# A transformer block on one core: the first stage put in program order on three engines, and a cleared scratch tile between scatters

## The chip, the cores and the metric

The kernel runs on one core of a Trainium2 chip. A core has five engines that work beside each other: TensorE (PE in the profile, with its weight load as PEld), VectorE (DVE), ScalarE (ACT), GpSimd (POOL) and SyncE (SP). Each takes its own instructions strictly in the order in which the build laid them out, and waits at an instruction until what it needs has been signalled. SyncE here only issues DMAs; GpSimd also issues the DMAs that scatter rows to computed addresses. PSUM is the memory that TensorE writes to, SBUF the one that all engines work in.

The metric is the device time of one execution in microseconds, and lower is better. Seven runs of the kernel before have a median of 507.76 us (505.48 to 509.74).

## What is computed

One block over 2048 tokens of width 256: an attention over a sliding window of 64, then a mixture of 16 experts with 4 chosen per token, each behind a layer norm that is shifted and scaled by a small product (`c` with `w_mod`).

```python
mod = (silu(c) @ wmod).reshape(1, 6, 1, -1)        # sa, ca, ga, sb, cb, gb
h = layernorm(x) * (1 + ca) + sa
q, k, v = split(h @ w_qkv.T)                       # 16 heads of 16
s = q k^T / 4 over chunks of 64 queries, 128 keys  # this chunk and the one before, masked
x = x + ga * (softmax(s) @ v) @ w_out.T
h = layernorm(x) * (1 + cb) + sb
probs = softmax(abs((h @ ru.T) * silu(h @ rg.T)))  # 16 experts
idx = top 4 of probs + extra_bias;  w = 1 + probs[idx] * extra_scale[idx]
y = sum over the 4 experts: w * ((silu(h @ Wg.T) * (h @ Wu.T)) @ Wd.T)
z = (silu(h @ Sg.T) * (h @ Su.T)) @ Sd.T           # the shared expert
x = x + gb * (y + z)
```

## The kernel before

**Tiles.** The tokens are cut into four blocks of 512 (NB = 4, TB = 512), each of four tiles of 128 (NT). The width of 256 is two halves of 128 (KC = 2).

**First stage.** All loads are issued on SyncE at L263 to L287, in the order of the lines: `c`, block 0 of x, the first third of w_mod, the weights of queries, keys and values, the rest. A one-time fill of constants (masks, identity, counters) runs on VectorE and GpSimd at L114 to L187. `shift_scale` (L299) makes shift and scale of a norm by eight small matmuls (two passes each) into `ps_mod` and two VectorE copies into `mod`.

**front(b)** (L352) prepares a block: `norm_t` (L227) takes four bn_stats and bn_aggr on VectorE (L233, L234), a square root on ScalarE (L236), four normalisations `xn` (L241), eight transposes on TensorE (L249) and two ScalarE passes into `hT` (L250); then come queries (L363, split into even and odd heads by VectorE at L368 and ScalarE at L369), keys (L374, copied by ScalarE at L378) and values (L393, copied at L397 to L399). It is a generator: each `yield` is a point at which the loop that drives it turns to something else.

**Attention** runs over 64 units (16 for a block, UNITS), driven by the loop at L692. A unit is one of four head pairs of a half block. `scores(u)` (L443) fills PSUM for two units, mask first (L450), then eight products (L456). `softmax(u)` takes the row maximum on VectorE (`top`, L472). Even units subtract it there (L482) and take one Exp on ScalarE (L485); odd ones take four Exps with a bias and a running sum (L477). `total` sums the even ones (L490), `turn_p` transposes (L497, copied by L499), and once in four units `spread`, `turn_s`, `values` and `heads_out` make the weighted values (L507, L519, L533, L546). While a block's units run, the loop advances by one step per unit `front` of the next block and `back` of the one before; `gates` takes the place of `back` in the first block.

**back(b)** (L556) applies the output weights (`ps_a`), adds to x (L569), does the second norm into a tile `row` (two buffers), routes (L581 to L658) and appends 16 entries to `sends`: four choices times four tiles.

**send** (L664) takes one entry: a GpSimd copy into the last column of the row's tile, from an operand that VectorE has written (`tops` of the unit two ahead in the loop; in the tail of the stage a result of the shared expert), and then a scatter of 128 rows to `slots` in HBM (L673). The copy is there only to hold the scatter back: the column is spare. A copy into a row waits until the scatter that last read that tile has landed.

**After the last unit** the expert weights `wgu` (5632 KB) are loaded over the attention's buffers (L724). The shared expert of blocks 0 to 2 (`shared`, L403, driven by `beside`) covers the rest of routing. Then the fill counts are known (`ps_n`, L747), SyncE writes 16 blank tiles behind the filled slots (L805) and loads the rows of each expert tile (`xr`, L820); the first of these loads waits for every scatter and every blank. The shared expert of block 3 runs meanwhile. 79 expert tiles follow, each with transposes, two products and an accumulating scatter (L831 to L878), and at the end the sums are loaded, added to x and stored.

**Order.** A scheduler in the build, which weighs readiness and program order by its own estimates, decides the order on each engine. Nothing in the kernel before overrides it.

Of the kernel before, what the change touches and what calls it, by code (L numbers as in the profile page):

```python
# [8 lines left out]
F32 = mybir.dt.float32  # L9
BF16 = mybir.dt.bfloat16  # L10
# [7 lines left out]
P = 128  # L18
E = 256
KC = E // P  # L20
HD = 16
W = 64
TB = 512
NT = TB // P
# [6 lines left out]
def adaln_block_kernel(  # L31
# [17 lines left out]
    nc = tc.nc  # L49
    S = x.shape[0]  # L50
    NB = S // TB
# [11 lines left out]
    RW = E + NE + 4  # L63
# [9 lines left out]
    xs = []  # L73
# [37 lines left out]
        return w.rearrange("(k p) n -> p k n", p=P)  # L111


    ident = const.tile([P, P], F32, name="ident")  # L114
    make_identity(nc, ident)
    eps_b = const.tile([P, 1], F32, name="eps_b")
# [110 lines left out]
    def norm_t(pool, psum, xb, half, dst, xn=None):  # L227

        mv = pool.tile([P, NT, 2], F32, tag="mv", name="mv")
        rstd = pool.tile([P, NT], F32, tag="rstd", name="rstd")  # L230
        for t in range(NT):
            st = pool.tile([P, 6], F32, tag="st", name="st")
            nc.vector.bn_stats(st, xb[:, t, :])  # L233
            nc.vector.bn_aggr(mv[:, t, :], st)  # L234
        yield
        nc.scalar.activation(rstd, mv[:, :, 1], AF.Sqrt, bias=eps_b[:, 0:1])  # L236
        nc.vector.reciprocal(rstd, rstd)
        if xn is None:
            xn = pool.tile([P, NT, E], F32, tag="xn", name="xn", bufs=1)
        for t in range(NT):  # L240
            nc.vector.tensor_scalar(  # L241
                xn[:, t, :], xb[:, t, :], mv[:, t, 0:1], rstd[:, t : t + 1],
                ALU.subtract, ALU.mult,
            )
        for k in range(KC):
            yield
            ps = psum.tile([P, NT, P], F32, tag="mm", name="ps_xt")
            for t in range(NT):
                nc.tensor.transpose(ps[:, t, :], xn[:, t, k * P : (k + 1) * P], ident)  # L249
            nc.scalar.activation(  # L250
                dst[:, k, :], ps[:, :, :].rearrange("p t q -> p (t q)"), AF.Identity,
                bias=mod[:, 3 * half, k : k + 1], scale=mod[:, 3 * half + 1, k : k + 1],
            )
# [87 lines left out]
    with ExitStack() as actx:  # L341
# [6 lines left out]
        k_before = None  # L348
# [3 lines left out]
        def front(b):  # L352
            nonlocal k_before, ve_next
            yield from norm_t(wa, ps_mm, xs[b], 0, hT[b])


            qz = next(q_ring).rearrange("p (k n h q) -> p k n h q", k=KC, h=2, q=W)
            kT = next(k_ring).rearrange("p (k n) -> p k n", k=KC)
            for m in range(KC):
                yield  # L360
                ps = ps_mm.tile([P, TB], F32, tag="mm", name="ps_q")
                for k in range(KC):
                    nc.tensor.matmul(  # L363
                        ps, lhsT=wqkv[:, k, m * P : (m + 1) * P], rhs=hT[b][:, k, :],
                        start=(k == 0), stop=(k == KC - 1),
                    )
                by_chunk = ps[:, :].rearrange("p (n q) -> p n q", q=W)
                nc.vector.tensor_scalar(qz[:, m, :, 0, :], by_chunk, parity[:, 0:1], None, ALU.mult)  # L368
                nc.scalar.mul(qz[:, m, :, 1, :], by_chunk, parity[:, 1:2])  # L369
            for m in range(KC):  # L370
                yield
                ps = ps_mm.tile([P, TB], F32, tag="mm", name="ps_k")
                for k in range(KC):
                    nc.tensor.matmul(  # L374
                        ps, lhsT=wqkv[:, k, E + m * P : E + (m + 1) * P], rhs=hT[b][:, k, :],
                        start=(k == 0), stop=(k == KC - 1),
                    )
                nc.scalar.copy(kT[:, m, W:], ps)  # L378
            if k_before is None:
                nc.vector.memset(kT[:, :, 0:W], 0.0)  # L380
            else:
                nc.vector.tensor_copy(kT[:, :, 0:W], k_before[:, :, TB:])
            k_before = kT


            window = []
            for t in range(NT):
                yield
                vo = next(v_ring["vo"])
                ve, ve_next = ve_next, next(v_ring["ve"])  # L390
                ps = ps_mm.tile([P, E], F32, tag="mm", name="ps_v")
                for k in range(KC):
                    nc.tensor.matmul(  # L393
                        ps, lhsT=hT[b][:, k, t * P : (t + 1) * P], rhs=wqkv[:, k, 2 * E :],
                        start=(k == 0), stop=(k == KC - 1),
                    )
                nc.scalar.copy(vo, ps)  # L397
                nc.vector.tensor_copy(ve[W:P], ps[0:W])
                nc.vector.tensor_copy(ve_next[0:W], ps[W:P])  # L399
                window += [ve, vo]  # L400
            heads[b] = qz, kT, window

        def shared(b, hidden, psum):  # L403

            hs = []
            for j in range(SJ):
                n = min(P, SH - j * P)
                h = hidden()
                hs.append(h)
                pg, pu = psum(), psum()  # L410
                for ps, w in ((pg, sg), (pu, su)):
                    for k in range(KC):
                        nc.tensor.matmul(  # L413
                            ps[0:n], lhsT=w[:, k, j * P : j * P + n], rhs=hT[b][:, k, :],
                            start=(k == 0), stop=(k == KC - 1),
                        )
                    yield hs[-2][:, 0:1] if j else None
                nc.scalar.activation(h[0:n], pg[0:n], AF.Silu)
                nc.vector.tensor_tensor(h[0:n], h[0:n], pu[0:n], ALU.mult)
            for t in range(NT):  # L420
                ps = psum()[:, 0:E]
                for j in range(SJ):
                    n = min(P, SH - j * P)
                    nc.tensor.matmul(  # L424
                        ps, lhsT=hs[j][0:n, t * P : (t + 1) * P], rhs=sd[0:n, j, :],
                        start=(j == 0), stop=(j == SJ - 1),
                    )
                nc.vector.tensor_tensor(xs[b][:, t, :], ps, xs[b][:, t, :], ALU.add)
                yield xs[b][:, t, 0:1]

        UNITS = 4 * 2 * KC
        probs, tops, sums, turned, scale, av, outs = {}, {}, {}, {}, {}, {}, {}

        def where(u):

# [24 lines left out]
        def softmax(u):  # L464

            g, r = divmod(u, 4)
            s = probs[u]
            if r == 0:
                sums[g] = wa.tile([P, 4, 4], F32, tag="sum", name="sum")
            alone = r % 2 == 1  # L470
            top = tops[u] = wa.tile([P, 4], F32, tag="top", name="top", bufs=6)
            nc.vector.tensor_reduce(top, s, AX.X, ALU.max, negate=alone)  # L472
            sm = wa.tile([P, 4, 2 * W], F32, tag="sm", name="sm", bufs=4)
            probs[u] = sm
            if alone:
                for n in range(4):
                    nc.scalar.activation(  # L477
                        sm[:, n, :], s[:, n, :], AF.Exp, bias=top[:, n : n + 1],
                        accum_out=sums[g][:, n, r : r + 1],
                    )  # L480
                return
            nc.vector.tensor_tensor(  # L482
                sm, s, top[:, :].unsqueeze(2).to_broadcast([P, 4, 2 * W]), ALU.subtract
            )
            nc.scalar.activation(sm, sm, AF.Exp)  # L485
# [175 lines left out]

        sends = []

        def send(after=None):  # L664

            at, row, t, i = sends.pop(0)  # L670
            if after is not None:
                nc.gpsimd.tensor_copy(row[0 : after.shape[0], t, RW - 1 : RW], after)  # L672
            ins = nc.gpsimd.indirect_dma_start(  # L673
                out=slots[:, :],
                out_offset=bass.IndirectOffsetOnAxis(ap=at[:, t, i : i + 1], axis=0),
# [5 lines left out]


        heads = {}
        shift_scale(ps_mm, 0)
        for _ in front(0):
            pass
        last = NB * UNITS
        scores(0)
        softmax(0)
        softmax(1)  # L690
        nexts, ends = iter(()), gates(wa, ps_mm)
        for u in range(last + 3):  # L692
            if u % UNITS == 0 and u // UNITS + 1 < NB:
# [24 lines left out]
            next(nexts, None)  # L718
            for _ in range(2 if r == 3 else 1):
                next(ends, None)  # L720

            for _ in range(min(len(sends), 2 if r == 3 else 1)):
                send(tops[min(u + 2, last - 1)][:, 0:1])
        nc.sync.dma_start(out=wgu, in_=w_gu_t.rearrange("(k p) e n -> p k e n", p=P))  # L724


# [8 lines left out]
        side = beside()  # L735
        for _ in ends:
            next(side, None)
            done = next(side, None)
            for _ in range(min(len(sends), 2)):
                send(done)  # L740
        while sends:
            done = next(side, None)
            send(done)


        ps = ps_mm.tile([P, NE], F32, tag="mm", name="ps_n")
# [224 lines left out]
```

## Time and profile before

The profiled execution took 507.14 us, of which 505.4 us are the span from its first to its last instruction.

| what | value |
|---|---|
| median of 7 runs | 507.76 us |
| profiled execution, its span | 507.14 us, 505.4 us |
| TensorE busy | 459.5 us (91%) |
| VectorE busy | 337.9 us (67%) |
| ScalarE busy | 226.3 us (45%) |
| GpSimd busy | 203.0 us (40%) |
| first row maximum (`top`) starts | 29.12 us |
| `wgu` load issued | 213.97 us |
| first expert product (`pgu`) | 284.02 us |
| granted TensorE clock, mean | 0.972 |

A timeline row reads: start in us, busy us, engine, line and operation, what is written from what, shapes, count; in brackets the idle time of the engine just before the row and what ended it. A row of the windows reads: the stretch and its length, then busy us of PE, PEld, DVE, ACT and POOL with the number of instructions in brackets, the granted TensorE clock, the busy share of the DMA engines and GB/s. Times of an engine in a row overlap at their edges, so that rows back to back start closer together than they last.

### The profile page before, as it was taken

The numbers are of one execution on the slowest core, as the hardware profiler recorded it, in microseconds if no ns is written. First come the engines' busy times: TensorE is split into PE (matmuls) and PEld (weight loads), VectorE is DVE, ScalarE is ACT, GpSimd is POOL, SyncE is SP. The second block draws the span as 40 slices with busy tenths as digits, with TensorE's granted clock in tenths as the row PEclk, the third lists the DMA queues.
The fourth block names the chain that finished last, engine by engine and source line by source line (L and its number), as shares of the span: only waits on it lengthen the run. The fifth ranks groups of instructions, "written<-read, shape, count | busy, mean of one in ns | idle before, by whom it ended". The sixth has DMA issues, their size and how long they took to land.

```text
span 505.4 us, 9573 instructions
## 1 busy us (share of the span) xinstructions
PE 459.5 (91%) x2921; PEld 324.1 (64%) x2921; DVE 337.9 (67%) x913; ACT 226.3 (45%) x623; POOL 203.0 (40%) x224
## 2 busy tenths in 40 slices
PE   3999979998998899899999999999999999999900
PEld 3575757666766677556553777777777777777700
DVE  5599789789969898755324466666666666666625
ACT  2377687958866868733001233333333333333200
POOL 2002000007701750246363066566666556666630
PEclk9999999999999899899999999999999999999965
DMA  8978000002200220095126487777777657665478
GB/s 281 320 153 285 21 1 3 0 1 82 92 10 12 91 80 2 23 408 195 46 90 224 102 150 131 114 112 117 104 116 108 105 104 111 118 100 58 57 217 314
DMA packets 52565, 58.88 MB, mean 117 GB/s; under 512 B 16363, under 2 KB 48331, under 8 KB 52171
## 3 DMA queue, kind: packets, MB, share of 16 engines
q1 hardware_dynamic: 36435, 35.72, 24.8%
q0 software_dynamic: 14448, 19.41, 22.3%
q10 hardware_dynamic: 1632, 3.15, 1.6%
q8 instruction: 24, 0.39, 0.3%
q14 instruction: 26, 0.21, 0.2%
HBM read 29.90 MB, written 28.35 MB: 115 GB/s over the span
## 4 chain that ended last, share of the span: by engine, by line
PE 42%; DMA 37%; DVE 12%; ACT 4%; issue 3%; DVEq 0%; SPq 0%; POOLq 0%; ACTq 0%
DMA sum<-y,xr 34%; PE pz L413 8%; PE pz L424 4%; PE pt L497 4%; PE s L456 3%; DVE top L472 3%; PE ps_q L363 3%; PE av L533 3%; PE pgu L849 2%; PE ps_a L564 2%; PE ps_k L374 2%; DMA got<-sum 2%; ACT sm L477 2%; PE s L450 2%; PE ps_xt L249 1%
## 5 line engine op out<-in xcount | busy, mean ns | idle before, releaser
L878 POOL DMA_INDIRECT sum<-y,xr x79 | 122.2, 1547 | 92.1 <-DVE y L877 34.4
L849 PE MATMUL pgu<-wgu,xT 128*128 x316 | 106.5, 460 | 0.4 <-DVE xT L837 0.4
L871 PE MATMUL py<-wd,hT 88*128 x316 | 81.4, 379 | 0.1
L673 POOL DMA_INDIRECT slots<-row,at x64 | 63.4, 991 | 32.5 <-POOL row L672 13.6
L833 ACT ACTIVATE xT<-px,mod 128x128 f32<-128x128 f32 x79 | 36.1, 457 | 81.1 <-PE px L831 80.9
L849 PEld LDWEIGHTS pgu<-wgu,xT 128*128 128x128 f32 x316 | 53.8, 190 | 17.4 <-ACT xT L833 0.6
L865 DVE COPY hT<-ph 88x256 f32<-88x256 f32 x79 | 33.2, 421 | 39.8 <-PE ph L863 39.8
L871 PEld LDWEIGHTS py<-wd,hT 88*128 88x128 f32 x316 | 53.6, 190 | 4.8 <-DVE hT L865 0.5
L672 POOL COPY row<-top 128x1 f32<-128x1 f32 x44 | 8.3, 200 | 110.0 <-DVE sr L606 62.2
L855 ACT ACTIVATE h<-pgu 128x176 f32<-128x176 f32 x79 | 25.1, 318 | 59.3 <-PE pgu L849 59.3
L477 ACT ACTIVATE sm<-s,top 128x128 f32<-128x128 f32 x128 | 45.8, 371 | 11.1 <-DVE top L472 11.0
L497 PE MATMUL pt<-ident,sm 128*128 128x128 f32 x256 | 41.3, 284 | 7.3 <-ACT sm L485 6.0
L837 DVE TENSOR_SCALAR xT<-px,mod 128x128 f32<-128x128 f32 x79 | 32.4, 410 | 22.0 <-ACT xT L833 21.9
L499 ACT COPY pT<-pt 128x512 f32<-128x512 f32 x64 | 37.5, 593 | 19.8 <-PE pt L497 19.4
L472 DVE TENSOR_REDUCE top<-s 128x4 f32<-128x512 f32 x64 | 42.2, 683 | 3.2 <-PE s L456 2.8
L456 PEld LDWEIGHTS s<-wgu 32*128 32x128 f32 x512 | 31.7, 186 | 15.9 <-issue 15.5
L877 DVE TENSOR_TENSOR y<-py,gate 128x256 f32<-128x256 f32 x79 | 33.6, 425 | 11.7 <-PE py L871 1.0
L497 PEld LDWEIGHTS pt<-ident,sm 128*128 128x128 f32 x256 | 29.3, 143 | 15.6 <-ACT sm L485 6.9
L456 PE MATMUL s<-wgu 32*128 32x128 f32 x512 | 38.9, 285 | 0.0
L863 PEld LDWEIGHTS ph<-ident,h 128*88 128x88 f32 x158 | 19.4, 123 | 21.9 <-issue 13.5
L856 DVE SCALAR_TENSOR_TENSOR h<-h,by,pgu 128x176 f32<-128x176 f32 x79 | 30.3, 384 | 1.3 <-ACT h L855 1.3
L831 PE MATMUL px<-ident,xr 128*128 128x128 f32 x158 | 30.4, 273 | 0.1
(169 smaller groups left out, 710.0 us busy)
## 6 DMA issues: line engine op xcount, KB each, us to landing
xr<-slots SPq DMA_DIRECT2D x79, 138.0 KB, 2.6
wgu<-in_w_gu_t SPq DMA_DIRECT2D x1, 5632.0 KB
sum<-blank SPq DMA_DIRECT2D x2, 2176.0 KB
wd<-in_w_down_t SPq DMA_DIRECT2D x1, 2816.0 KB
slots<-blank SPq DMA_DIRECT2D x17, 138.0 KB, 2.4
x<-in_x SPq DMA_DIRECT2D x4, 512.0 KB
got<-sum SPq DMA_DIRECT2D x4, 512.0 KB, 6.9
got<-sum ACTq DMA_DIRECT2D x4, 512.0 KB
```

The lines of the kernel that those rows point to most:

```text
L413: nc.tensor.matmul(ps[0:n], lhsT=w[:, k, j * P : j * P + n], rhs=hT[b][:, k, :], start=(k == 0), stop=(k == KC - 1),)
L456: nc.tensor.matmul(probs[u + i][:, n, :], lhsT=qz[at, m, ch].rearrange("p h q -> p (h q)"), rhs=kT[at, m, ch * W : (ch + 2) * W], start=False,
L472: nc.vector.tensor_reduce(top, s, AX.X, ALU.max, negate=alone)
L477: nc.scalar.activation(sm[:, n, :], s[:, n, :], AF.Exp, bias=top[:, n : n + 1], accum_out=sums[g][:, n, r : r + 1],)
L497: nc.tensor.transpose(pt[:, n, :], p[:, n, :], ident)
L499: nc.scalar.copy(turned[u], pt)
L673: ins = nc.gpsimd.indirect_dma_start(out=slots[:, :], out_offset=bass.IndirectOffsetOnAxis(ap=at[:, t, i : i + 1], axis=0), in_=row[:, t, ...
L833: nc.scalar.activation(xT[b][:, 0, :], ps[:, 0, :], AF.Identity, bias=mod[:, 3, 0:1], scale=mod[:, 4, 0:1],)
L849: nc.tensor.matmul(ps, lhsT=xT[b][:, k, :], rhs=wgu[:, k, bass.ds(e, 1), :].rearrange("p e n -> p (e n)"), start=(k == 0), stop=(k == KC - 1),
L871: nc.tensor.matmul(ps, lhsT=hT2[b][:, c2, :], rhs=wd[:, c2, bass.ds(e, 1), :].rearrange("p e n -> p (e n)"), start=(c2 == 0), stop=(c2 == 1),)
L877: nc.vector.tensor_tensor(y, ps, gate[:, 1, :], ALU.mult)
L878: nc.gpsimd.indirect_dma_start(out=sums_of[b % NA][:, :], out_offset=bass.IndirectOffsetOnAxis(ap=xr[b][:, E + NE : E + NE + 1].bitcast(I3 ...
```

## The change

There are two parts.

The first stage, from the identity to the values of block 0, is built under a manual schedule for TensorE, VectorE and ScalarE, which keeps its instructions in program order on these three engines. The program's order is changed with it: two steps of `front(0)` (the norm) come before `shift_scale`; then the transposes, queries of half 0 and keys of half 0; then `scores(0)`, `softmax(0)` and `softmax(1)`; then queries and keys of half 1 and all values. In `front` the loops over queries and keys become one loop over halves, for every block. The bn_stats of the first norm of blocks 1 to 3 are kept in program order as well.

In `send` the copied operand is replaced: with `paced` set, GpSimd clears a scratch tile of 128 x 1024 bf16 (one buffer) and copies two of its columns into the spare column of two of the row's four tiles, t and the one two away from it. The last loop sends without pacing. `tops` is no longer kept, and its tile has four buffers in place of six.

```diff
+    first_order = ctx.enter_context(ExitStack())
+    first_order.enter_context(tc.manual_schedule(
+        engines={mybir.EngineType.PE, mybir.EngineType.DVE, mybir.EngineType.Activation}
+    ))
     ident = const.tile([P, P], F32, name="ident")
...
-            nc.vector.bn_stats(st, xb[:, t, :])
+            ins = nc.vector.bn_stats(st, xb[:, t, :])
+            if half == 0 and xb is not xs[0]:
+                tc.keep_in_program_order(ins)
...
+            if k_before is None:
+                nc.vector.memset(kT[:, :, 0:W], 0.0)
+            else:
+                nc.vector.tensor_copy(kT[:, :, 0:W], k_before[:, :, TB:])
+            k_before = kT
+            window = []
+            heads[b] = qz, kT, window
             for m in range(KC):
...
                 nc.scalar.mul(qz[:, m, :, 1, :], by_chunk, parity[:, 1:2])
-            for m in range(KC):
                 yield
                 ps = ps_mm.tile([P, TB], F32, tag="mm", name="ps_k")
...
-            top = tops[u] = wa.tile([P, 4], F32, tag="top", name="top", bufs=6)
+            top = wa.tile([P, 4], F32, tag="top", name="top", bufs=4)
...
-        def send(after=None):
+        def send(paced):
             at, row, t, i = sends.pop(0)
-            if after is not None:
-                nc.gpsimd.tensor_copy(row[0 : after.shape[0], t, RW - 1 : RW], after)
+            if paced:
+                pause = wa.tile([P, 1024], BF16, tag="pause", name="pause", bufs=1)
+                nc.gpsimd.memset(pause, 0.0)
+                nc.gpsimd.tensor_copy(row[:, t % 2 :: 2, RW - 1], pause[:, 0 : NT // 2])
...
+        starts = front(0)
+        next(starts)
+        next(starts)
         shift_scale(ps_mm, 0)
-        for _ in front(0):
-            pass
-        last = NB * UNITS
+        for _ in range(KC + 2):
+            next(starts)
         scores(0)
         softmax(0)
         softmax(1)
+        for _ in starts:
+            pass
+        first_order.close()
+        last = NB * UNITS
...
-                send(tops[min(u + 2, last - 1)][:, 0:1])
+                send(True)
...
-            done = next(side, None)
+            next(side, None)
             for _ in range(min(len(sends), 2)):
-                send(done)
+                send(True)
         while sends:
-            done = next(side, None)
-            send(done)
+            next(side, None)
+            send(False)
```

More of the change, by code (lines that the diff above doesn't have):

```diff
@@ L378, in front @@
                 nc.scalar.copy(kT[:, m, W:], ps)
[L379 to L386, printed above, removed]
             for t in range(NT):
@@ L400, in front @@
                 window += [ve, vo]
-            heads[b] = qz, kT, window
         def shared(b, hidden, psum):
@@ L416, in shared @@
                         )
-                    yield hs[-2][:, 0:1] if j else None
+                    yield
                 nc.scalar.activation(h[0:n], pg[0:n], AF.Silu)
@@ L428, in shared @@
                 nc.vector.tensor_tensor(xs[b][:, t, :], ps, xs[b][:, t, :], ALU.add)
-                yield xs[b][:, t, 0:1]
+                yield
         UNITS = 4 * 2 * KC
-        probs, tops, sums, turned, scale, av, outs = {}, {}, {}, {}, {}, {}, {}
+        probs, sums, turned, scale, av, outs = {}, {}, {}, {}, {}, {}
         def where(u):
```

## The prediction

> **What bounds the kernel now.** I read the page's shares first, then the windows, then the timeline of the first 36 us and of the hand-over to the experts. TensorE is busy 91% of the span. From the end of attention (about 215 us) it runs with hardly a gap through the shared expert into 79 expert tiles, and only the last 21 us are without it. Whatever moves the end of attention therefore moves the end of the kernel one for one, as long as the first `xr` load is there when the shared expert ends.
>
> In attention three engines share the limit, and which of them binds changes every ten microseconds:
>
> ```profile
> PE 459.5 (91%) x2921; PEld 324.1 (64%) x2921; DVE 337.9 (67%) x913; ACT 226.3 (45%) x623; POOL 203.0 (40%) x224
> ...
> 70.00:75.00 5.00, 3.23 (x49) 2.79 (x52) 4.14 (x8) 3.54 (x13) 0.00 (x0) 1.00 0.01 3
> 75.00:80.00 5.00, 5.00 (x58) 4.03 (x49) 4.59 (x9) 3.73 (x13) 0.00 (x0) 1.00 0.00 0
> 85.00:90.00 5.00, 4.44 (x46) 2.30 (x46) 4.60 (x13) 3.86 (x8) 0.00 (x0) 1.00 0.03 7
> 120.00:125.00 5.00, 3.99 (x47) 2.94 (x49) 4.67 (x11) 4.33 (x16) 4.27 (x8) 1.00 0.27 97
> 125.00:130.00 5.00, 5.00 (x66) 4.06 (x55) 4.75 (x10) 3.96 (x14) 4.13 (x7) 1.00 0.31 106
> ```
>
> Third and fifth figure are busy TensorE and VectorE. At 120 to 125 us TensorE idles 1.01 us while VectorE idles 0.33: there VectorE's work sets the pace. Such stretches are where added VectorE work costs time.
>
> The start, before the first softmax:
>
> ```profile
> 6.32 3.54 PE L304 MATMUL ps_mod<-sc,hT 128*128 128x1 f32 x16 [6.32 <-DVE st L233]
> 9.90 0.16 DVE L310 COPY mod<-ps_mod 128x2 f32<-128x2 f32 x1 [3.39 <-PE ps_mod L304]
> 10.04 0.24 DVE L234 BATCH_NORM_AGGREGATE mv<-st 128x2 f32<-128x6 f32 x2
> 10.32 0.30 ACT L236 ACTIVATE rstd<-mv,eps_b 128x4 f32<-128x4 f32 x1 [6.20 <-DVE mv L234]
> 14.20 1.45 ACT L250 ACTIVATE hT<-ps_xt,mod 128x512 f32<-128x512 f32 x2 [3.59 <-PE ps_xt L249]
> 15.45 4.10 PE L363 MATMUL ps_q<-hT,wqkv 128*128 128x512 f32 x8
> 22.11 0.30 ACT L236 ACTIVATE rstd<-mv,eps_b 128x4 f32<-128x4 f32 x1
> 27.14 0.30 ACT L236 ACTIVATE rstd<-mv,eps_b 128x4 f32<-128x4 f32 x1
> 28.15 1.28 ACT L477 ACT_TABLE_LOAD   x1
> 29.12 1.29 DVE L472 TENSOR_REDUCE top<-s 128x4 f32<-128x512 f32 x2
> ```
>
> Two aggregates stand behind the copy that waits for `ps_mod` (9.90), so the norm ends late and queries start at 15.45. From there TensorE is busy to 35 us with hardly a gap. The square roots at 22.11 and 27.14 belong to blocks 1 and 2: the scheduler has pulled two norms ahead of the first Exp table load (28.15), into time in which VectorE waits for TensorE anyway.
>
> **The change, part by part** (minus is faster).
>
> *Start.* The new VectorE order has all constants first, then the four statistics, and the `mod` copies last. The mask is there at about 3.1 us; some 25 small operations at their spacing of about 0.1 take 2.9, to 6.0; four statistics with aggregates 2.0 (two pairs take 0.87 at 20.25); square root 0.30 and reciprocal 0.18; four `xn` 1.4: 9.9, when `ps_mod` ends too (6.32 + 3.54). Eight transposes take 1.1 to 2.1, `hT` ends at about 12.3 instead of 15.65: 3.3 gained. Then:
> - four mask products (0.63 each at first, 0.38 later) filled TensorE's wait for `hT`. Now they stand behind the first keys: 1.3 lost;
> - queries need both `hT` halves: 0.5 of waiting;
> - ScalarE takes the Exps of units 0 and 1 ahead of the second half's query and key passes. The maximum of unit 0 ends at 18.6, the last of the two Exp groups at 21.4, then 0.69 + 0.59: keys at 22.7, while TensorE is done with them at 21.5: 1.2 lost;
> - `ps_gate` takes the PSUM buffer of the fourth value tile, whose VectorE copies now stand behind a maximum that itself waits for scores issued after `ps_mod`: 1.5 lost.
>
> That eats the 3.3 to -1.2. What comes back is block 2's norm, no longer in front of units 4 to 7: by walking the two orders on to the scores of unit 8 (45.7 before) I get about 45.0. I take -0.7, between -3.4 (all of the lead) and +1.0.
>
> *Norms of blocks 2 and 3.* Kept in program order, they move one block later: block 2's from 22 to 49 us to between maxima 19 and 22 (73 to 80 us), block 3's from 82 to 100 us to between maxima 35 and 38 (124 to 130 us). A norm is 1.74 (four pairs) + 0.1 + 1.28 = 3.1 us of VectorE. Block 2's: VectorE idles 0.86 + 0.41 in 70 to 80, so up to 1.8 are uncovered, against up to 0.56 of TensorE idle that goes at 85 to 90; bounds 0 and +1.8, taken +1.0. Block 3's: VectorE idles 0.33 + 0.25 in 120 to 130, so up to +2.5; the lower bound is the boundary at 85 to 90, which carried two norms in the kernel before and cost TensorE 0.56. I take +1.7, nearer the stretch it lands in.
>
> *Table loads.* A square root amid Exps costs two loads: 1.28 + 0.30 + 1.28 (rows at 83.42, 84.72, 86.98). The ScalarE order has two such groups more, 5.7 us. Upper bound +5.7; the loads at 83 and 87 hid within an idle 1.00, so the lower is 0. ScalarE idles 0.67 and 1.04 in 120 to 130: I take +0.8.
>
> *Scatters.* 58 copies become 48 copies and 48 clears. A clear is not in the trace; the bf16 clears of 512 and 128 columns took 0.52 and 0.20 us, so 0.83 ns a column and 0.95 for 1024; bounds 0.52 and twice that, 1.04. A paced send is 0.19 copy + 0.28 + 0.98 scatter + 0.95 + 0.1 = 2.5 us against 1.6:
>
> ```profile
> 119.42 0.19 POOL L672 COPY row<-top 128x1 f32<-128x1 f32 x1
> 119.89 1.13 POOL L673 DMA_INDIRECT slots<-row,at  x1 [0.28 <-POOL row L672]
> 121.03 0.19 POOL L672 COPY row<-top 128x1 f32<-128x1 f32 x1
> ...
> DMA to landing us min/median/max: 9.7/11.1/12.5
> ...
> 267.09 10.42 SPq L805 DMA_DIRECT2D slots<-blank  x16
> 279.44 0.37 SPq L820 DMA_DIRECT2D xr<-slots  x1
> ...
> 282.68 0.93 PE L831 MATMUL px<-ident,xr 128*128 128x128 f32 x4
> ```
>
> Blocks 0 and 1 send in 40 us, well before `row` is wanted again (routing points lie 48 us apart). Block 2's collide with the `wgu` load from 214 us, in which a scatter lands after 11 us (fourth row). A copy now waits for the scatter two back, not four. Walked: third scatter 215.3, fourth 217.5, fifth 226.6, sixth 228.8, seventh 232.3; nine more at 2.5 end at 254.8; block 3's sixteen at 1.3 end at 275.6 and land by 278.2. The first `xr` load waits at 279.4 for the blanks in any case, so this lies 1.2 inside its cover. The cover is thin, as TensorE takes `xr` at 282.68 with nothing to spare: +0.3, bounds 0 and +3.6 (cycle 2.8, seventh scatter 2 us later).
>
> *Port.* VectorE's copy of `taken` took 0.53 us at 2.04 us, when GpSimd was busy, and 0.16 at 210.02: at most 0.4 lost per meeting. About 15 such small copies lie within the clears' stretches, with 0.38 of the time cleared: 15 x 0.38 x 0.4 = 2.3 at most, 0 at least, since VectorE often waits; +0.2. [...] No run here shows a clear of this length beside VectorE.
>
> Other edits cost nothing: four `top` buffers still cover the two units that are in flight; the blank write now leaves SyncE behind the `sd` loads and about 1 us later, with block 1's x wanted only at 21 us.
>
> Sum: -0.7 + 1.0 + 1.7 + 0.8 + 0.3 + 0.2 = **+3.3**. On the profiled execution 507.14 + 3.3 = 510.4. That run lies 0.62 under the median of 507.76, which gives **511.0**.
>
> **The rivals.** A measurement of this kernel can tell about 0.5% (2.5 us) from no change.
> 1. *Faster*: the lead of `hT` lives on. TensorE has work for every microsecond of the start, and VectorE loses block 2's norm just where it is saturated (9.62 of 10 us at 35 to 45). If the maximum of unit 8 starts by 44.4 instead of 47.74 and the norms fall into TensorE-bound time, it is 507.76 - 3.4 = 504.4. Against it: VectorE and ScalarE still have the same gates and copies ahead of that unit.
> 2. *Same*: both boundaries behave as 85 to 90 us does, 0.56 each, and the loads hide: -0.7 + 1.1 = +0.4, 508.2. For it: that boundary did carry two norms. Against: it had them where TensorE was about to be bound.
> 3. *Slower still*: scatters decide. If block 2's run past 258 us, the first `xr` is late: 511.0 + 3.3 = 514.3.
> 4. *It does not do what it says*: GpSimd's order has the first two clears and copies of each block hoisted ahead, so that two scatters a block go unpaced. This belongs to the sum already and moves no more than 0.3.
>
> **How the numbers follow.** Forecast (slower by norms and loads, around 511.0) 0.34; rival 3 0.11; rival 2 0.28; rival 1 0.27. So faster 0.27, same 0.28, slower 0.45. Range: down to 503.5, a microsecond past rival 1's time, and up to 515.5, a microsecond past rival 3's; the forecast's own range is 509 to 514.
>
> **What would show it.** `hT` of block 0 ends near 12.3 and the first maximum starts near 17.9. The scores of unit 8 start at 45.0, give or take 1. TensorE idles more than before around maxima 19 to 22 and 35 to 38, by 1 to 2 us each. Seven square-root loads lie ahead of the shared expert, where there were five. The last scatter ends near 276 and the first `xr` load is issued as the blanks land. The forecast is wrong if unit 8 is reached 3 us earlier or those boundaries add no idle time.

## The result, and the profile after

The changed kernel takes 520.49 us (median of 19 runs, 515.80 to 526.64), the kernel before 507.83 (46 runs beside them, 505.48 to 512.31): a ratio of 1.0228, 95% interval 1.0208 to 1.0248. It is 12.7 us slower. Ratios, here and below, leave out executions over 1.5% longer than the fastest of their kernel, so a ratio need not be the quotient of the medians. I had said 511.0, with a range up to 515.5: the sign was right, and the loss was nearly four times the one I had summed. The profiled execution has a span of 521.3 us (505.4 before) and a mean granted TensorE clock of 0.959 (0.972 before).

The page after; in the group, the second line, busy us, mean ns and idle us stand behind the bars:

```profile
PE 471.1 (90%) x2921; PEld 332.5 (64%) x2921; DVE 345.8 (66%) x913; ACT 232.0 (44%) x627; POOL 248.2 (48%) x262
...
L679 POOL MEMSET pause<- 128x1024 bf16 x48 | 46.7, 972 | 0.4
```

The same work keeps TensorE busy 11.6 us longer and VectorE 7.9. The 48 clears make up the 45 us that GpSimd gained. The granted clock fell, and the windows show where (it is the third figure from the end):

```profile
35.00:40.00 5.00, 5.00 (x22) 4.18 (x22) 4.83 (x12) 2.39 (x3) 0.00 (x0) 0.67 0.49 108
70.00:75.00 5.00, 3.46 (x40) 2.48 (x36) 4.71 (x10) 3.33 (x12) 0.00 (x0) 1.00 0.02 3
75.00:80.00 5.00, 3.85 (x44) 3.38 (x44) 3.87 (x10) 3.96 (x13) 0.00 (x0) 0.66 0.00 0
125.00:130.00 5.00, 3.25 (x35) 2.40 (x37) 4.11 (x9) 3.57 (x13) 3.74 (x7) 1.00 0.15 57
130.00:135.00 5.00, 5.00 (x69) 3.78 (x64) 5.00 (x14) 4.59 (x14) 4.06 (x6) 1.00 0.18 61
135.00:140.00 5.00, 4.20 (x19) 3.01 (x18) 5.00 (x11) 2.86 (x7) 4.05 (x5) 0.73 0.15 57
200.00:205.00 5.00, 5.00 (x30) 4.09 (x29) 2.33 (x4) 4.17 (x13) 3.81 (x6) 0.50 0.09 35
```

The stretch from 75 to 80 us had a clock of 1.00 and TensorE without a gap before; now it has 0.66. A stretch at half clock (called a drop from here on) lasts 3.4 us or a multiple up to the end of attention in these traces: there the drops sum to 20.5 us after and 6.8 before. From 130 to 140 us VectorE has no idle time at all; there block 3's norm has landed.

The timeline after, at the start, at that norm and at the hand-over:

```profile
3.15 1.65 DVE L144 COPY mask<-mask 64x512 bf16<-64x512 bf16 x1 [0.59 <-POOL mask L140]
...
3.71 0.94 POOL L679 MEMSET pause<- 128x1024 bf16 x1
...
5.24 0.95 POOL L679 MEMSET pause<- 128x1024 bf16 x1
5.25 1.02 DVE L148 CAST ident_b<-ident 128x128 bf16<-128x128 f32 x1
...
7.75 3.57 PE L311 MATMUL ps_mod<-sc,hT 128*128 128x1 f32 x16 [7.75 <-DVE sc L297]
...
12.89 1.63 ACT L257 ACTIVATE hT<-ps_xt,mod 128x512 f32<-128x512 f32 x2 [2.20 <-PE ps_xt L256]
13.72 3.78 PE L377 MATMUL ps_q<-hT,wqkv 128*128 128x512 f32 x4
...
21.45 0.69 DVE L478 TENSOR_REDUCE top<-s 128x4 f32<-128x512 f32 x1 [3.15 <-PE s L462]
...
135.88 2.52 DVE L248 TENSOR_SCALAR xn<-x,mv,rstd 128x256 f32<-128x256 f32 x4
136.29 0.98 POOL L679 MEMSET pause<- 128x1024 bf16 x1
...
294.93 0.37 SPq L833 DMA_DIRECT2D xr<-slots  x1
...
297.13 0.44 PE L844 MATMUL px<-ident,xr 128*128 128x128 f32 x2 [1.30 <-DMA xr<-slots]
```

The mask copy and the cast in the timeline before:

```profile
10.43 0.22 DVE L143 CAST ident_b<-ident 128x128 bf16<-128x128 f32 x1
...
11.63 0.29 DVE L139 COPY mask<-mask 64x512 bf16<-64x512 bf16 x1
```

Now the first two clears, which the scheduler has hoisted to the start, lie beside them: the copy ends 0.15 us behind the first clear, the cast 0.08 behind the second. `sc`, which `ps_mod` waits for, stands behind both. The norm at 135.88 is held in the same way: the first of its four operations takes 1.53 us in place of 0.41 and ends 0.15 us behind the clear. At the end TensorE waits 1.30 us for `xr`, where it had nothing to wait for before.

How far each kernel lies behind the kernel before (start of the row maximum of that number, us), with the half-clock time up to the last one:

| kernel | max. 8 | 16 | 24 | 32 | 40 | 48 | 63 | half clock |
|---|---|---|---|---|---|---|---|---|
| before | 0 | 0 | 0 | 0 | 0 | 0 | 0 | 6.8 |
| after | 2.7 | 3.1 | 4.9 | 5.1 | 9.8 | 10.6 | 13.0 | 20.5 |
| e9 (tail paced) | 3.5 | 3.9 | 5.8 | 6.0 | 9.0 | 9.2 | 9.1 | 17.1 |
| e11 (e9, no kept norms) | 7.1 | 7.6 | 8.9 | 9.3 | 9.6 | 10.4 | 9.5 | 13.7 |
| e12 (block 3's norm free) | 2.4 | 2.8 | 2.5 | 6.7 | 9.0 | 8.2 | 7.9 | 20.5 |
| e10 (clears alone) | 1.9 | 1.9 | 3.3 | 3.3 | 3.5 | 3.8 | 3.3 | 10.2 |
| e17 (e10, later gate) | 0.9 | 0.6 | 0.6 | 0.6 | 1.0 | 1.0 | 0.8 | 6.8 |
| e18 (e9, split gate) | 2.7 | 3.2 | 3.5 | 3.8 | 8.6 | 9.4 | 9.3 | 10.2 |

### The profile page after: what moved, and what is told of

Read it like the earlier page. It is cut to its first block, busy times and chain, and to the rows that moved or that the text cites. A ratio compares the mean times of both kernels' runs of the same rounds, so it can differ in the third digit from the quotient of the medians.

```text
span 521.3 us, 9596 instructions
## 1 busy us (share of the span) xinstructions
PE 471.1 (90%) x2921; PEld 332.5 (64%) x2921; DVE 345.8 (66%) x913; ACT 232.0 (44%) x627; POOL 248.2 (48%) x262
## 4 chain that ended last, share of the span: by engine, by line
PE 28%; DMA 22%; POOL 4%; issue 4%; DVE 3%; DVEq 0%; SPq 0%; ACT 0%; POOLq 0%; ACTq 0%
DMA sum<-y,xr 14%; PE pgu L862 12%; PE py L884 8%; DMA slots<-row,at 6%; POOL slots L681 3%; PE px L844 2%; PE ph L876 2%; DMA got<-sum 2%; POOL pause L679 1%; PE pt L503 1%; PE s L462 1%; DMA xr<-slots 0%; DVEq L980 0%; PE ps_r L590 0%; DVE sum L496 0%
## 5 line engine op out<-in xcount | busy, mean ns | idle before, releaser
L681 POOL DMA_INDIRECT slots<-row,at x64 | 64.5, 1008 | 117.8 <-DVE at L664 81.5
L478 DVE TENSOR_REDUCE top<-s 128x4 f32<-128x512 f32 x64 | 42.5, 680 | 10.6 <-PE s L462 10.4
L679 POOL MEMSET pause<- 128x1024 bf16 x48 | 46.7, 972 | 0.4
L462 PEld LDWEIGHTS s<-wgu 32*128 32x128 f32 x512 | 35.2, 190 | 18.1 <-issue 17.6
L505 ACT COPY pT<-pt 128x512 f32<-128x512 f32 x64 | 36.8, 589 | 15.0 <-PE pt L503 14.7
L462 PE MATMUL s<-wgu 32*128 32x128 f32 x512 | 43.3, 290 | 0.0
L890 DVE TENSOR_TENSOR y<-py,gate 128x256 f32<-128x256 f32 x79 | 33.6, 425 | 11.5 <-PE py L884 0.8
L503 PEld LDWEIGHTS pt<-ident,sm 128*128 128x128 f32 x256 | 30.9, 149 | 13.8 <-ACT sm L491 7.5
```

The source lines that it names most:

```text
L462: nc.tensor.matmul(probs[u + i][:, n, :], lhsT=qz[at, m, ch].rearrange("p h q -> p (h q)"), rhs=kT[at, m, ch * W : (ch + 2) * W], start=False,
L503: nc.tensor.transpose(pt[:, n, :], p[:, n, :], ident)
L505: nc.scalar.copy(turned[u], pt)
L679: nc.gpsimd.memset(pause, 0.0)
L681: ins = nc.gpsimd.indirect_dma_start(out=slots[:, :], out_offset=bass.IndirectOffsetOnAxis(ap=at[:, t, i : i + 1], axis=0), in_=row[:, t, ...
```

## Experiments

The runs fell into two groups: A, in which the kernel before takes 508 to 509 us (the measurement above, e9 to e12, e17, e18), and B, in which it takes 529 to 530 (the others). Each ratio is to the kernel before, measured on the same chip at the same time. What makes the difference is not known. The record numbers the chips 11 (e9 to e12) and 15 (e17, e18) in A, and 2 (e1 to e4), 1 (e5 to e8) and 15 (e13 to e16) in B; with 15 in both, A and B need not be two kinds of chip.

### The parts one by one (B)

**e1**: kept norms alone. **e2**: the new `send` alone. **e3**: the changed kernel without the kept norms. **e4**: the changed kernel with the old `send`.

```diff
e1, on the kernel before
+            ins = nc.vector.bn_stats(st, xb[:, t, :])
+            if half == 0 and xb is not xs[0]:
+                tc.keep_in_program_order(ins)
e2, on the kernel before
+                pause = wa.tile([P, 1024], BF16, tag="pause", name="pause", bufs=1)
+                nc.gpsimd.memset(pause, 0.0)
+                nc.gpsimd.tensor_copy(row[:, t % 2 :: 2, RW - 1], pause[:, 0 : NT // 2])
e3, on the changed kernel
-            if half == 0 and xb is not xs[0]:
-                tc.keep_in_program_order(ins)
e4, on the changed kernel
-                nc.gpsimd.memset(pause, 0.0)
+                nc.gpsimd.tensor_copy(row[0 : after.shape[0], t, RW - 1 : RW], after)
```

> The kernel before with one edit: the bn_stats of the first norms of blocks 1 to 3 are kept in program order. Theory N (the norms kept in program order are most of the loss, with the square-root table loads that come with them): block 2's norm lies between maxima 19 and 22, block 3's between 35 and 38, as in the changed kernel, so two of its three jumps return (4.6 us at the third to fourth group of units, 7.9 at the seventh to eighth, of a lag of 13.0 at the end of attention): 516 to 520. Theory S (the clears between the scatters are most of the loss): within 2 us of the kernel before. Theory F (the first stage's order is most of it): within 2 us of the kernel before, the norms hide behind TensorE as they did at maxima 22 to 26.

> The kernel before with the other half of the change alone: GpSimd's clear and two-column copy between scatters, four buffers for the row maximum, nothing of the first stage. Theory S: the clears hold VectorE's small copies and the last block's scatters end late, 514 or more. Theory N: attention ends within 2 us of before; what is left is block 2's scatters, which end late by 1 to 3 us for the first load of expert rows: 508 to 511.

> The changed kernel without the line that keeps the bn_stats of blocks 1 to 3 in program order: the scheduler pulls the norms of blocks 1 and 2 ahead of the first row maximum again and that of block 3 to maxima 22 to 26. Theory N: the jumps at the third to fourth and the seventh to eighth group of units go, 508 to 512. Theory S: 517 or more. Theory F: 515 or more, with the lag there before maximum 16.

> The changed kernel with the sends of the kernel before (no clears, copies of operands that VectorE has written, six buffers for the row maximum). Theory N: 516 to 520, as the kernel with the norms kept alone, and what is missing to the changed kernel's 520.5 is the late first load of expert rows, 1 to 3 us. Theory S: within 3 us of the kernel before.

Measured: e1 537.6 us, 1.0147 (1.0081 to 1.0214); e2 524.0, 0.9901 (0.9863 to 0.9939); e3 529.3, 1.0008 (0.9974 to 1.0042); e4 533.8, 1.0078 (1.0044 to 1.0113); the kernel before 528.8. By the sizes no theory fits: e2, with the clears, is faster, and the kernel before is 21 us slower than in the first measurement. So I ran both kernels themselves and two more combinations.

### Both kernels themselves, and two combinations (B)

**e5** and **e6** are unchanged. **e7** has the first stage alone (manual schedule, new order of steps, merged loop), **e8** the clears and the kept norms without the first stage.

> The kernel before, unchanged, run as a kernel of its own so that its trace can be laid beside those of the runs here: on the chip that ran the four kernels so far it took 528.8 us against 507.8 where the change was first measured. If TensorE stands still between the count of the rows and the first load of expert rows, as it did for 10.2 and 6.6 us in the two kernels with the clears and without the kept norms, the extra 21 us lie there; if not, they lie in attention, as half-clock stretches of TensorE (3.4 us each).

> The changed kernel, unchanged, for its trace and its time on the same chip as the others. Theory N: 1.0 to 2.3 per cent slower than the kernel before on this chip too, the loss at the block boundaries. If the loss belonged to one chip, no difference here.

> The kernel before with the first stage of the changed kernel alone: manual order on three engines, the new order of steps and the merged loop over halves; no kept norms, the old sends. Theory N: the first maximum comes 3 to 8 us earlier, the lead is gone by unit 16, and the time is within 2 us of the kernel before. Theory F: 4 us or more slower.

> The kernel before with the clears and the kept norms, and its own first stage. Theory N: as the kernel with kept norms alone, plus 0 to 3 us for the late scatters: 1.5 to 2.5 per cent slower than the kernel before. If clears and kept norms were independent, the ratio is the product of the two single ones, 0.990 x 1.015 = 1.005.

Measured: e5 529.5 us, 0.9998 (0.9960 to 1.0037); e6 532.9, 0.9991 (0.9950 to 1.0032); e7 534.4, 1.0087 (1.0044 to 1.0130); e8 534.1, 1.0054 (1.0006 to 1.0102). e7 is 4.6 us slower by its ratio, as theory F has it, and its trace is 8.0 behind at maximum 16 where e5's is 2.6. e8's ratio is about the product of those of e1 and e2, 1.005. e1 and e8 lose most where theory N did not look: they are 9.5 and 6.7 behind at maximum 8 (e5 2.6). In e1 TensorE waits 1.50 us for `xn` of block 1 at 43.3 us, and a drop of 10.2 us follows at 45.4; e8 has one as long at 42.3.

On B the change costs nothing that shows, since both kernels lose there: e5 is 15.8 us behind at the last maximum, and e6 takes 89.8 us from there to the first `px`, where A's kernel before takes 75.0. The timeline of e5, the kernel before on B:

```profile
120.67 1.08 PE L533 MATMUL av<-pT,wgu 128*32 128x128 f32 x32
...
126.27 0.69 DVE L546 TENSOR_TENSOR prod<-av,by 128x512 f32<-128x512 f32 x1 [3.71 <-PE pt L497]
```

`av` is shown done at 121.75, and VectorE gets it 4.5 us later. e5 and e2 have the same order on TensorE, VectorE and ScalarE; both are 3.9 us behind A's kernel before at maximum 24, but at the last e5 is 15.8 behind and e2 4.3. The 11.5 us between them are steps of 3 to 3.6 us beside the old sends. What e2 wins there it pays at the hand-over (timeline of e2):

```profile
280.66 0.97 POOL L675 DMA_INDIRECT slots<-row,at  x1 [0.31 <-issue]
284.52 0.41 DVE L782 CAST table<-ps_b 1x256 int32<-1x256 f32 x1 [10.92 <-remote]
284.60 0.60 ACT L418 ACTIVATE hs<-pz 128x512 f32<-128x512 f32 x1 [21.21 <-remote]
```

VectorE and ScalarE stand still until 3.9 us after the last unpaced scatter starts, and TensorE for 10.2 us with them.

### The tail, and the parts on A

**e9** is the changed kernel with the tail paced as before; **e10** the kernel before with the clears in the attention loop only; **e11** is e9 without the kept norms; **e12** the changed kernel with block 3's norm left free. **e16** is e10 once more, on B.

```diff
e9, on the changed kernel; e10 and e16 have the same tail
-            next(side, None)
-            send(False)
+            done = next(side, None)
+            send(False, done)
e12, on the changed kernel
-            if half == 0 and xb is not xs[0]:
+            if half == 0 and (xb is xs[1] or xb is xs[2]):
```

> The changed kernel, except that the sends behind the last unit are held back as in the kernel before, by a copy of a result of the shared expert (the clears stay in the attention loop). Question: what the tail's unpaced scatters cost. Theory H (the sixteen unpaced scatters of block 3 hold TensorE up at the hand-over): on a chip where the kernel before takes 529 us, the standstill of about 10 us between the count of the rows and the first load of expert rows goes, and the time is 8 to 11 us below the changed kernel; on a chip where it takes 508, no standstill was there, and the time is within 3 us of 520. If the standstill comes from the late scatters of block 2 alone, nothing changes on either.

> The kernel before, except that the copy of a row maximum in the attention loop is replaced by the clear and the two-column copy; the tail is held back as before, and nothing of the first stage or of the norms is touched. Theory N: on a chip where the kernel before takes 508 us, attention ends within 2 us of it and the time is 506 to 511. On one where it takes 529, TensorE's standstills of 3.5 to 8 us beside the old sends go from attention (11 us there in the two traces) and the one at the hand-over goes too: 513 to 518, faster than both kernels.

> The changed kernel with the paced tail and without the kept norms: what is left is the first stage and the clears in the loop. Theory N (the kept norms lose at each block boundary): 5 to 9 us below the first of these kernels at the end of attention behind block 1, but its first stage starts later by the two early norms, so the lag at maximum 8 is about 7 us; the time is 2 to 6 us below that kernel. If the kept norms cost nothing on this chip: equal within 2 us.

> The changed kernel with the norms of blocks 1 and 2 kept in program order and that of block 3 free: the scheduler puts its statistics between maxima 24 and 26, where block 2's are in no kernel. Theory N: the lag to the kernel before up to maximum 24 is as in the changed kernel; the step between maxima 36 and 46 (5 to 7 us in the traces of the changed kernel) shrinks to under 2, or comes at maxima 24 to 32 instead. 3 to 7 us below the changed kernel if it shrinks.

> The kernel with the clears in the attention loop and the tail held back as before, once more. On a chip where the kernel before takes 529 us: 513 to 518, no standstill at the hand-over. On one where it takes 508: 513 again, with half-clock stretches near 31 and 75 us that the kernel before does not have, though no scatter is sent before 114 us.

Measured on A: e9 521.8 us, 1.0252 (1.0186 to 1.0318); e10 513.0, 1.0083 (1.0054 to 1.0111); e11 519.8, 1.0208 (1.0164 to 1.0251); e12 521.9 (four runs from 514.3 to 530.8, no ratio); the kernel before 509.4. On B: e16 514.7, 0.9692 (0.9646 to 0.9738), with no standstill: in the timeline of e16,

```profile
274.36 0.41 DVE L784 CAST table<-ps_b 1x256 int32<-1x256 f32 x1 [0.47 <-PE ps_b L782]
274.44 0.60 ACT L418 ACTIVATE hs<-pz 128x512 f32<-128x512 f32 x1 [10.55 <-PE ps_b L782]
```

So on B the standstill belongs to the unpaced tail (the programs of e2 and e16 differ in nothing but the tail's sends; the chips were 2 and 15), and e16 beats both kernels there. On A no such standstill exists: from the last maximum to the first `px` the changed kernel takes 76.4 us there, e2 88.5 on B; and e9 stays within 3 us of 520, as theory H has it. Theory N is not borne out by e11: taking the kept norms away wins 2.0 us, where N's range begins and that of no cost ends, within the intervals, and at the last maximum e11 is no less behind than e9. The table shows why: it loses the early start (7.1 behind at maximum 8, against 3.5) and wins the boundaries back (from maximum 32 to 40, 0.3 in place of 3.0). e12 loses 4.2 us from maximum 24 to 32 and 2.3 from 32 to 40, where the changed kernel loses 0.2 and 4.7: moved, not won.

e10 is the surprise. It has the order of the kernel before on TensorE, VectorE and ScalarE, and its first scatter is sent after 114 us; yet it is 1.9 behind at maximum 8 and 3.3 at 24. In its timeline and windows:

```profile
29.18 2.04 PE L304 MATMUL ps_mod<-sc,hT 128*128 128x1 f32 x16
31.09 3.56 PE L322 MATMUL ps_gate<-hT,sc_rows 128*128 128x256 f32 x8
```

```profile
30.00:35.00 5.00, 5.00 (x24) 4.30 (x24) 4.31 (x10) 2.65 (x10) 0.00 (x0) 0.66 0.75 154
75.00:80.00 5.00, 4.84 (x53) 3.93 (x56) 3.16 (x6) 4.24 (x16) 0.00 (x0) 0.66 0.00 0
```

In the timeline before:

```profile
30.58 1.97 PE L322 MATMUL ps_gate<-hT,sc_rows 128*128 128x256 f32 x8
```

The lag is 0.4 at the start, 1.5 more at the first drop and 1.4 at the second, and in the table it stays between 3.3 and 3.8 from maximum 24 on, where nearly all the clears lie.

### Is it the place of the work against the clock? (B)

**e13**, **e14**, **e15**: the kernel before, 1, 2 and 4 small loads later.

```diff
+    late = const.tile([P, 2, KC], F32, name="late")
+    for i in range(2):
+        nc.sync.dma_start(out=late[:, i, :], in_=c)
     nc.sync.dma_start(out=c_sb, in_=c)
```

> The kernel before with one small load (1 KB) more ahead of the first loads on SyncE, which delays them by about 0.45 us; a few of the first constants and mask products change places, from the queries on the order is the same on TensorE, VectorE and ScalarE. Theory C (the granted clock depends on where low-activity stretches fall against a grid of 3.4 us): the time grows by 0.45 plus 0 to 4 us, and what lies beyond the delay shows as steps of 1 to 1.7 us at half-clock stretches. Rival (the clock follows the order of the work): +0.45 us, half-clock stretches where the kernel before has them.

> As the kernel with one small load more, with two: delay about 0.9 us. Theory C: 0.9 plus 0 to 4 us, not the same surplus as with one. Rival: +0.9.

> As the kernel with one small load more, with four: delay about 1.85 us. Theory C: 1.85 plus 0 to 4 us, not the same surplus as with one or two. Rival: +1.85.

Measured: 530.2 us, 1.0022 (0.9983 to 1.0060); 533.1, 1.0026 (0.9991 to 1.0061); 534.4, 1.0074 (1.0035 to 1.0112). The times can't separate the theories on B, but the traces do up to maximum 31, ahead of B's own losses. e13 lies 1.0 us behind from the first maximum to that one: no drop, no step. e14 starts 1.5 behind, with drops at 32 and 76 us and steps of 1.5 and 1.3. e15 starts 4.7 behind, with one drop and one step of 1.5. From the queries on the three engines' order is the same up to there. The windows of e13 and of e14:

```profile
30.00:35.00 5.00, 4.95 (x35) 4.29 (x35) 4.97 (x11) 3.66 (x13) 0.00 (x0) 1.00 0.81 169
75.00:80.00 5.00, 4.84 (x67) 3.98 (x67) 4.60 (x10) 4.39 (x14) 0.00 (x0) 1.00 0.00 0
```

```profile
30.00:35.00 5.00, 5.00 (x29) 4.34 (x28) 4.96 (x11) 3.57 (x11) 0.00 (x0) 0.71 0.75 162
75.00:80.00 5.00, 4.03 (x44) 3.41 (x44) 2.58 (x5) 4.35 (x16) 0.00 (x0) 0.66 0.00 0
```

That is theory C as far as the steps go: the same work in the same order loses 0, 1.5 or 2.8 us. The delay does not set it: e5, 1.1 us late, has both drops. The place against the clock's own steps fits. In every trace all drops start a multiple of 3.413 us apart, so they give a grid. This is how far the next edge of that grid lies behind the start of the first row maximum, in all traces with the order of the kernel before from the queries to maximum 31 (e17, below, has the gate's products later):

| trace | before | e13 | e17 | e16 | e2 | e10 | e14 | e5 | e15 |
|---|---|---|---|---|---|---|---|---|---|
| edge, us | 0.98 | 1.04 | 1.08 | 1.30 | 1.35 | 1.37 | 1.45 | 1.64 | 2.66 |
| drops before 100 us | 0 | 0 | 0 | 2 | 2 | 2 | 2 | 2 | 1 |

The drops sort by this place. It was worked out after the runs, from nine traces, and no run tested it.

### Can the first drop be taken away? (A)

**e17** is e10, **e18** is e9, each with shift and scale of the second norm in two tiles and a step between them.

```diff
-        shift_scale(psum, 1)
-        yield
+        for i in range(2):
+            ps = psum.tile([P, KC], F32, tag="mm", name="ps_mod")
...
+            yield
```

> The kernel with the clears in the attention loop and the paced tail; shift and scale of the second norm get a PSUM tile each, with a step of the loop between them, and the gate's products come two units later. Theory L (a stretch of one-column products and what follows is counted as low activity): no half-clock stretch near 31 us, the step of 1.5 us at maximum 4 goes, 511 to 513. Rival (the place of the grid alone decides): the stretch stays or goes as the grid falls, and the time stays at 513 to 515.

> The changed kernel with the paced tail and the same split; its eight one-column products of each half now have four score products between them. Theory L: no half-clock stretch at 32 to 38 us, where the same kernel without the split had 6.8 us of it: 1.5 to 3 us less than its 521.8 on a chip where the kernel before takes 508. Rival: no systematic change.

Measured: e17 510.6 us, 1.0044 (0.9999 to 1.0088); e18 520.9, 1.0241 (1.0135 to 1.0347); the kernel before 508.4. e17 has neither early drop and lies 0.6 to 1.0 us behind all through attention, clears and all. But its sixteen one-column products still stand in one piece (the scheduler put them together; only `ps_gate` moved), and e18, where they are split, still drops at 34.3 us. Theory L is not shown: e17's edge lies at 1.08 in the table above, beside the two traces without early drops, so the place can account for its clock without theory L.

## Why the prediction was wrong

- **The granted clock was not in the sum.** This is the step that failed most. I took every matmul at the duration of the kernel before. Over the 17 runs of the changed kernel that its ratio counts, the time goes with the clock lost, (1 - clock) x span, at 0.75 us per us (correlation 0.79); the median lost is 20.7 us, against 14.7 for the kernel before (22 runs on A). That makes an estimate of 0.75 x 6.0 = 4.5 of the 12.7 us; by the slope of those 22 runs, 1.12, it would be 6.7. The profiled run has 13.7 us of half clock more, at most 6.8 us.
- **Start, -0.7.** Lag 3.1 at maximum 16; without the one drop there (1.5 a drop in e10 and e14) it is +1.6. `hT` ends at 14.52, not 12.3. I let the constants end at 6.0; the two hoisted clears hold two VectorE copies for 1.36 + 0.80 = 2.2 us, and `ps_mod` starts at 7.75 instead of 6.32. In e4, the same first stage without clears, it starts at 6.6 and `hT` ends at 12.77, near my 12.3: so the clears cost `hT` about 1.7 us. I had rival 4's hoisting move no more than 0.3. The four queries then took 0.95 each, not 0.5: the trace's clock record begins, at full speed, at 17.9 us, before at 16.4, and what runs ahead of it is slow in both (a product of the queries takes 1.06 us ahead of it and 0.59 behind it). Part of this is clock again. In e6, the changed kernel itself, `hT` ends at the same time, but the record begins at 14.9 us and the first drop comes at 72.9:

```profile
12.88 1.63 ACT L257 ACTIVATE hT<-ps_xt,mod 128x512 f32<-128x512 f32 x2 [2.19 <-PE ps_xt L256]
13.71 2.56 PE L377 MATMUL ps_q<-hT,wqkv 128*128 128x512 f32 x4
...
19.98 0.69 DVE L478 TENSOR_REDUCE top<-s 128x4 f32<-128x512 f32 x1 [2.91 <-PE s L462]
```

Its lag at maximum 16 is 0.5, ahead of what it loses on B (17.1 us of half clock from 195.8 on). So of the 1.6 some 1.1 are the late rise of the clock, and 0.5 is order.

- **Block 2's norm, +1.0.** e18, with no drop between maxima 16 and 24, gives +0.3; in its bounds.
- **Block 3's norm, +1.7, and table loads, +0.8.** From maximum 24 to 40 the changed kernel loses 4.9 and e18 5.1, each with one drop: some 3.5 without it, against 2.5. The seven square-root loads came as said. The rest fits the clear that holds `xn` for 1.1 us where VectorE has no idle time, in the changed kernel's one trace. e4, the same norm beside old sends:

```profile
138.54 1.36 DVE L248 TENSOR_SCALAR xn<-x,mv,rstd 128x256 f32<-128x256 f32 x4
```

- **Port, +0.2.** Mis-sized. VectorE is busy 337.4 us in e4 and 345.8 with the clears, 8.4 more; I had bounded it by 2.3, from small copies alone. The longest single operations are `row` (1.73 us), routing's `at` (1.69), the mask copy (1.65) and `xn` (1.53); routing's small operations together make up about half. The mask copy ends only behind the whole clear beside it, and takes 1.65 us in place of 0.29. Here the earlier start spared neither: the copy and `xn` start 0.56 and 0.41 us ahead of their clears and end 0.15 behind them, beside GpSimd work that runs up to the clears. In the old place of the norms it hardly matters: e17 has the clears and is 0.8 us behind at the end of attention. By these runs the cost comes of clears together with a norm moved into their stretch and constants moved beside them.
- **Scatters, +0.3, and rival 3.** A paced send took 2.77 us, not 2.5, and block 2's went on to 271, past 258 even when the 13.0 us of delay are taken off. From the last maximum to the first `px` it took 75.0 us before and 76.4 after: 1.4, where rival 3 put 3.3 more on the forecast. e9 and e18, paced, have 76.3 and 75.1, so the tail's part is not settled.

So of 12.7 us, as an estimate, some 5.6 are clock (4.5, and 1.1 by the late rise, which the record of the clock leaves out) and 7 are order with the clears: the start 0.5, the boundaries about 4, the hand-over 1.4, and about 1 behind it that I can't place. The sum of 3.3 had this part at less than half. What remains open is what in the work turns an edge of the grid into a drop, why A and B differ, and what delays TensorE's results on B.

## What to carry to other kernels

Compare the granted clock stretch by stretch before explaining a difference of a few us: here an unchanged order lost 0 to 2.8 by its place. Price a long GpSimd operation together with whatever the same change moves beside it, and look where the scheduler hoists it. When a wait is taken out of a tail, look at who else needs the machine there: pacing the tail made e16 9.3 us faster than e2, both on B.

## What the runs showed of the hardware

The half-clock stretches up to the end of attention last 3.413 us or a multiple. Against the start of the span their grid lies differently from trace to trace: in e13 to e15 an edge is 0.46, 1.34 and 2.37 us behind it, counted back in steps of 3.413. Yet from run to run the clock changed little on one chip (11): nine runs of the kernel before had 0.971 to 0.972, six of e10 0.965 to 0.968, which a grid that falls at random in each run would not lead one to expect. In the changed kernel the first drop (34.9 us) comes behind 14 us in which TensorE's rows show no gap, so no idle time just ahead of it accounts for that one. And the same kernel took 508 us in one group of runs and 529 in the other, while the kernel with the clears in its loop took 513 and 515.
